# Turning a batch's masks and weights with one transpose, and counting ranks by a scan on VectorE

## The chip, the cores and the metric

The kernel runs on one core of one Trainium2 chip. The metric is the device time of one execution in microseconds (us); the figure that counts is the median of three runs. Five engines work side by side: TensorE (PE; its weight loads are listed as PEld), VectorE (DVE), ScalarE (ACT), GpSimd (POOL) and SyncE (SP). ACT, SP and POOL also issue DMA transfers, each from its own queue.

## The reference

Two layers work on 32 batches of 128 tokens with 1024 features. In the first, each batch is multiplied by a 128x128 matrix that it picks, and the result goes through a mixture of 64 experts, of which each token takes eight. Every expert has room for 256 entries, filled in the order of the tokens:

```python
logits = x @ gate_w.T
w, sel = jax.lax.top_k(probs, K)              # K = 8 of E = 64
w = w / jnp.sum(w, axis=-1, keepdims=True)
oh = jax.nn.one_hot(eid, E, dtype=jnp.int32)
pos = jnp.sum(jnp.cumsum(oh, axis=0) * oh, axis=-1) - 1
valid = pos < CAP                             # CAP = 256
h = silu(inp @ wg) * (inp @ wu); out = h @ wd
```

The second layer is a linear map with adapters per batch and a mixture of eight small experts. The change doesn't touch it.

What matters here is `cumsum`: for each expert, the kernel has to know how many of the tokens up to a given one have chosen it. Together with the weight, that number is what finds the tokens of an expert later.

## The kernel before

The work runs in three stages. **Stage A** (to about 194 us) goes through the 32 batches. For batch `b`, `mixed(b)` multiplies it by its matrix on PE into two `ph` banks, which ACT copies to `hT`; `as_rows(b-1)` turns the batch before it on DVE; `stored(b-1)` writes that to `hbuf` in DRAM from ACT's queue; `logits(b-2)` multiplies `hT` by the gate weights on PE into `plog`; `topped(b-3)` finds the eight largest on DVE. Batches are loaded six ahead by SP (`x`) and POOL (`w`). SP also copies the input to `ybuf`, and in between PE multiplies weights of the second layer (`pcw`, `pcx`, `pcy`, `pcv`). **Stage B** runs the 64 experts: POOL gathers their tokens from `hbuf` (`xin`), PE multiplies, POOL adds the results to `ybuf`. **Stage C** is the second layer.

Every four batches form a group `g` (0 to 7). `powers(g)` and `weights_of(g)` make the weights `wt` from the mask of chosen experts, and `counted(g)`, one iteration later, makes the counts:

- `pcnt`: a matrix of ones times the masks of the four batches gives the number of tokens per expert and batch; DVE adds it up in `upto`.
- for two batches at a time, a bank `prk` of 64 partitions (the experts) holds four blocks of 128 tokens. A product of the mask with `upon`, a fixed matrix of zeros and ones, gives the running count of each expert over the tokens of a batch in their true order; a transpose (a pass with the identity matrix `ident`) gives the weights with experts on partitions.
- ACT copies the bank to `rk_sb` and stores it in `ranks` in DRAM, one row of 2 x 128 numbers per expert and batch: counts first, weights second.

The tokens of a batch lie on the partitions in an order by quarters (token `4i + q` on partition `32q + i`); `upon` takes account of that.

After group 7, `looked_up` finds for each expert slot its batch and the rank sought in it; `fetched` (L307) reads the rows of `ranks` by an indirect DMA into `rkg`; `found` compares, counts and picks the weight; PE's `rows_spread` and DVE's `placed` turn the result into row numbers; and `gathered` (L383) fetches the tokens.

The order on each engine is written out by hand. The wrapper `InOrder` keeps every instruction in the order in which the program text issues it, which is why nearly all rows of the profile carry its line, L219. Each engine works through its own queue in order, and a DMA issue that waits holds up what stands behind it on the same engine. In `counted`, the ACT queue holds copy, store, copy, store; behind it stand the `hT` copies of the next batch. The transfers issued by SP and ACT share eight completion counters in turn.

Of the kernel before, what the change touches and what calls it, by code (L numbers as in the profile page):

```python
# [8 lines left out]
F32 = mybir.dt.float32  # L9
# [3 lines left out]
ALU = mybir.AluOpType  # L13
# [4 lines left out]
P = 128  # L18
# [4 lines left out]
E = 64  # L23
# [9 lines left out]
GB = 4  # L33
# [12 lines left out]
Q = 32  # L46
NQ = P // Q
# [4 lines left out]
def kernel(  # L52
# [22 lines left out]
    nc = tc.nc  # L75

    dram = ctx.enter_context(tc.tile_pool(name="dram", bufs=1, space=DRAM))
    const = ctx.enter_context(tc.tile_pool(name="const", bufs=1))
# [9 lines left out]
    ranks = dram.tile([E, NB + 1, 2, P], F32, name="ranks")  # L88
# [4 lines left out]
    ident = const.tile([P, P], F32, name="ident")  # L93
    make_identity(nc, ident)
    ones = const.tile([P, P], F32, name="ones")
# [5 lines left out]
    iota_t = const.tile([P, P], F32, name="iota_t")  # L101
    nc.gpsimd.iota(
        iota_t, pattern=[[1, P]], base=0, channel_multiplier=0, allow_small_or_imprecise_dtypes=True
# [17 lines left out]
    quad = const.tile([P, 1], F32, name="quad")  # L121
# [4 lines left out]
    inquad = const.tile([P, 1], F32, name="inquad")  # L126
    nc.vector.tensor_scalar(inquad, quad, -float(Q), pcol, ALU.mult, ALU.add)

    mytok = const.tile([P, 1], F32, name="mytok")
    nc.vector.tensor_scalar(mytok, inquad, float(NQ), quad, ALU.mult, ALU.add)  # L130
    upon = const.tile([P, P], F32, name="upon")
    nc.vector.tensor_scalar(upon, iota_t, mytok, None, ALU.is_ge)

    tokrow = const.tile([P, P], F32, name="tokrow")
    nc.gpsimd.iota(
# [64 lines left out]
    def multiplied(n, d, hw, left, pool, tag, pe):  # L200
        w = BLOCKS[n][1] - BLOCKS[n][0]
        pcw = pool.tile([P, 512], F32, name=f"pcw_{n}_{d}", tag=tag)[:, 0:w]
        for j in range(HC):
            if j == HC // 2:
                yield
            pe.matmul(pcw, left[d][:, j, :], hw[:, j, :], start=(j == 0), stop=(j == HC - 1))
        yield pcw
# [5 lines left out]
    class InOrder:  # L213
# [7 lines left out]
    dve, pe, act, pool, sync = (  # L221
        InOrder(e) for e in (nc.vector, nc.tensor, nc.scalar, nc.gpsimd, nc.sync)
    )
# [174 lines left out]
    pa_sm = ppool.enter_context(tc.tile_pool(name="pa_sm", bufs=3, space=PSUM))  # L398
    with (
# [1 line left out]
        tc.tile_pool(name="a6", bufs=6) as a6,  # L401
        tc.tile_pool(name="a2", bufs=2) as a2,
    ):
        xs, ws, hTs, hqs, plogs, tops, lefts_of, exs, masks, wts_of = ({} for _ in range(10))

        def loaded_batch(b):
            ws[b] = a6.tile([P, P], F32, name=f"w_{b}", tag="w_b")
# [53 lines left out]
        def topped(b):  # L461
            g, t = divmod(b, GB)
            if t == 0:
                tops[g] = a2.tile([P, GB, K], F32, name=f"top_{g}", tag="top")
                lefts_of[g] = a2.tile([P, GB, E], F32, name=f"left_{g}", tag="left")
            dve.max(tops[g][:, t, :], plogs[g][:, t, :])
            dve.match_replace(lefts_of[g][:, t, :], tops[g][:, t, :], plogs[g][:, t, :], LOW)
            if t == GB - 1:
                nmax = a2.tile([P, GB], F32, name=f"nmax_{g}", tag="nmax")
                dve.tensor_scalar(nmax, tops[g][:, :, 0], -1.0, None, ALU.mult)  # L470
                masks[g] = a2.tile([P, GB, E], F32, name=f"mask_{g}", tag="mask")
                dve.tensor_scalar(masks[g], lefts_of[g], LOW, None, ALU.is_equal)
                exs[g] = nmax

# [6 lines left out]
                )  # L481

        def weights_of(g):
            wt = a2.tile([P, GB, E], F32, name=f"wt_{g}", tag="wt")
            dve.tensor_tensor(wt, exs[g], masks[g], ALU.mult)
            wsum = a2.tile([P, GB], F32, name=f"wsum_{g}", tag="wsum")
            dve.tensor_reduce(wsum, wt, AX.X, ALU.add)
            rsum = a2.tile([P, GB], F32, name=f"rsum_{g}", tag="rsum")
            dve.reciprocal(rsum, wsum)
            dve.tensor_tensor(wt, wt, rsum.unsqueeze(2).to_broadcast([P, GB, E]), ALU.mult)  # L490
            wts_of[g] = wt

        def counted(g):
            mask, wt = masks[g], wts_of[g]
            pcnt = pf.tile([P, 512], F32, name=f"pcnt_{g}", tag="prow")
            pcnt = pcnt[:, 0 : GB * E].rearrange("p (t e) -> p t e", t=GB)
            pe.matmul(pcnt, ones, mask, start=True, stop=True)
            for t in range(GB):  # L500
                b = g * GB + t
                if b == 0:
                    dve.tensor_copy(upto[:, :, b], pcnt[:, t, :])
                else:
                    dve.tensor_tensor(upto[:, :, b], upto[:, :, b - 1], pcnt[:, t, :], ALU.add)
            for i in range(2):
                rk_sb = a2.tile([E, 2, 2, P], F32, name=f"rk_{g}_{i}", tag="rk")
                prk = pa_sm.tile([E, 2, 2, P], F32, name=f"prk_{g}_{i}", tag="sm")
                for t in range(2):
                    pe.matmul(prk[:, t, 0, :], mask[:, 2 * i + t, :], upon, start=True, stop=True)  # L510
                    pe.transpose(prk[:, t, 1, :], wt[:, 2 * i + t, :], ident)
                act.copy(rk_sb, prk)
                two = slice(g * GB + 2 * i, g * GB + 2 * i + 2)
                act.dma_start(ranks[:, two, :, :], rk_sb)


        def combined(n, d):
# [63 lines left out]
        for b in range(NB):  # L581
# [6 lines left out]
            if b >= 3:  # L588
                topped(b - 3)
            g, t = divmod(b - 7, GB)  # L590
            if t == 0 and g >= 0:
                powers(g)
                weights_of(g)
            elif t == 1 and g >= 0:
                counted(g)
# [21 lines left out]
            if b == 25:  # L617
# [5 lines left out]
                pool.dma_start(ranks[:, NB, :, :], pad)  # L623
        logits(NB - 2)
        counted(NB // GB - 2)
        as_rows(NB - 1)
        stored(NB - 1)
        topped(NB - 3)
        topped(NB - 2)
        last = pair_of_rows(c, rows, sums)  # L630
        next(last)
        logits(NB - 1)
        topped(NB - 1)
        powers(NB // GB - 1)
        weights_of(NB // GB - 1)
        for _ in last:
            pass
        counted(NB // GB - 1)
    part = {0: looked_up([0, 1, 2, 3])}
    fetched(part[0], 2 * NJ)  # L640
# [554 lines left out]
    sm = wts.tile([P, HC, I], F32, name="sm", tag="wu").rearrange("p j i -> p (j i)")  # L1195
# [49 lines left out]
    _, pcw = multiplied(2, HC, hw, lefts, pc_p, "pp", pe)  # L1245
# [140 lines left out]
```

## Time and profile before

| | |
|---|---|
| runs | 2674.31, 2676.79, 2680.87 us (median 2676.79) |
| profiled execution | 2673.54 us, of which the span is 2671.8 us |
| PE busy | 2647.0 us (99%) |
| DVE, ACT, POOL busy | 1867.4 (70%), 547.7 (20%), 1047.3 us (39%) |
| granted PE clock over the span | 0.997 |
| `prk` with `upon` | 64 passes, 323 ns median each |
| `prk` with `ident` | 32 passes, 300 ns median each |
| `rk` copies | 16, 578 ns median |
| `ranks` stores | 16 of 128 KB, 4.8 us median to landing |

Passes on PE overlap, so their own lengths are longer than the distance from one start to the next. A view named the chain follows the work that ended last back from the end; a wait is shown with what released it. A product in float32 appears as two passes, a transpose as one.

### The profile page before, as it was taken

How to read it: one execution, taken by the hardware profiler on the slowest of the kernel's cores; microseconds unless marked ns; L12 is line 12 of the kernel's file. 1: busy time of each engine (PE TensorE's matmuls, PEld its weight loads, DVE VectorE, ACT ScalarE, POOL GpSimd, SP SyncE). 2: the span in 40 equal slices, each digit the busy share in tenths (PEclk: the TensorE clock that was granted, in tenths of full speed). 3: DMA queues.
4: the chain of work that ended last, by engine and by line, in shares of the span. 5: the costliest groups of instructions: out<-in, count | busy, mean ns of one | idle time of the engine just before them, and what ended most of it. 6: DMA issues, size and time to landing. Idle time of an engine off the chain costs nothing.

```text
span 2671.8 us, 25499 instructions
## 1 busy us (share of the span) xinstructions
PE 2647.0 (99%) x8932; PEld 1509.6 (57%) x8932; DVE 1867.4 (70%) x3050; ACT 547.7 (20%) x1174; POOL 1047.3 (39%) x854
## 2 busy tenths in 40 slices
PE   8999999999999999999999999999999999999999
PEld 8985555555555555555555555555555655554554
DVE  4456888888888888888888888878776644444442
ACT  2331222222222222222222222222222100000000
POOL 3106545546455464555555555554441000000000
PEclk9999999999999999999999999999999999999999
DMA  9869788788787887887888878878877322222110
GB/s 349 322 233 369 223 253 264 235 255 265 233 260 249 247 265 232 265 255 240 262 244 251 254 247 250 254 248 250 252 228 211 78 67 67 67 67 67 57 41 33
DMA packets 126367, 568.43 MB, mean 213 GB/s; under 512 B 22928, under 2 KB 48528, under 8 KB 100384
## 3 DMA queue, kind: packets, MB, share of 16 engines
q1 hardware_dynamic: 65664, 383.16, 41.0%
q0 software_dynamic: 52384, 161.60, 24.1%
q10 hardware_dynamic: 8192, 22.06, 2.1%
q8 instruction: 71, 1.16, 0.2%
q14 instruction: 56, 0.46, 0.1%
HBM read 459.68 MB, written 123.83 MB: 218 GB/s over the span
## 4 chain that ended last, share of the span: by engine, by line
PE 96%; DMA 2%; DVE 1%; POOL 1%; issue 0%; SPq 0%; ACT 0%; DVEq 0%; ACTq 0%
PE px L219 27%; PE pr_c L219 18%; PE pv L219 12%; PE py L219 6%; PE ph L219 2%; PE plog L219 2%; PE pth L219 2%; DMA xin<-hbuf,slot_row 1%; PE pcw L219 1%; PE pcx L219 1%; PE prk L219 1%; DMA WB_b<-in_WB 1%; PE pmx L219 1%; PE pcv L219 0%; POOL xin L383 0%
## 5 line engine op out<-in xcount | busy, mean ns | idle before, releaser
L383 POOL DMA_INDIRECT xin<-hbuf,slot_row x512 | 611.5, 1194 | 172.8 <-issue 148.1
L959 POOL DMA_INDIRECT ybuf<-o,slot_tok x128 | 208.0, 1625 | 680.8 <-DVE o L219 229.3
L219 PE MATMUL pr_c<-BM,X 128*128 128x512 f32 x480 | 216.0, 598 | 0.0
L219 POOL DMA_INDIRECT ab<-in_AT,adapter_rows x32 | 36.1, 1128 | 430.7 <-ACT pxw L219 425.2
L307 POOL DMA_INDIRECT rkg<-ranks,row x128 | 153.2, 1197 | 87.6 <-DVE past L219 48.8
L219 PE MATMUL px<-wg,xT 128*128 128x384 f32 x512 | 186.2, 487 | 0.6 <-ACT G_sb L219 0.6
L219 PE MATMUL pv<-t,s 128*128 128x384 f32 x512 | 175.7, 487 | 0.0
L219 PE MATMUL px<-t,s 128*128 128x384 f32 x512 | 175.6, 487 | 0.0
L219 PE MATMUL px<-wu,xT 128*128 128x384 f32 x512 | 175.6, 486 | 0.0
L219 PE MATMUL pv<-wu,s 128*128 128x384 f32 x512 | 175.6, 486 | 0.0
L219 PE MATMUL py<-wg,xT 128*128 128x384 f32 x512 | 175.6, 487 | 0.0
L219 PE MATMUL px<-t,xT 128*128 128x384 f32 x512 | 175.6, 486 | 0.0
L219 DVE TENSOR_TENSOR t<-wu,wg 128x1536 f32<-128x1536 f32 x64 | 113.3, 1770 | 74.2 <-PE pv L219 74.2
L219 DVE STREAM_TRANSPOSE xT<-xin 128x1024 f32<-128x1024 f32 x128 | 151.6, 1220 | 12.9 <-DMA xin<-hbuf,slot_row 10.2
L219 ACT COPY u<-px 128x384 f32<-128x384 f32 x128 | 61.2, 478 | 434.1 <-PE px L219 434.1
L219 PEld LDWEIGHTS pr_c<-BM,X 128*128 128x128 f32 x480 | 89.9, 192 | 101.2 <-issue 101.2
L219 PEld LDWEIGHTS pv<-t,s 128*128 128x128 f32 x512 | 97.4, 190 | 80.8 <-issue 26.0
L219 PE MATMUL pr_c<-ts,ss 128*128 128x512 f32 x320 | 142.4, 593 | 0.0
L219 PEld LDWEIGHTS px<-t,s 128*128 128x128 f32 x512 | 97.5, 190 | 67.6
L219 PEld LDWEIGHTS px<-t,xT 128*128 128x128 f32 x512 | 97.5, 190 | 67.7
L219 PEld LDWEIGHTS py<-wg,xT 128*128 128x128 f32 x512 | 97.5, 190 | 67.7
L219 PEld LDWEIGHTS pv<-wu,s 128*128 128x128 f32 x512 | 97.4, 190 | 67.7
(1570 smaller groups left out, 4553.7 us busy)
## 6 DMA issues: line engine op xcount, KB each, us to landing
wd<-in_wd SPq DMA_DIRECT2D x64, 1536.0 KB, 8.2
wg<-in_wg SPq DMA_DIRECT2D x63, 1536.0 KB, 8.1
wu<-in_wu SPq DMA_DIRECT2D x63, 1536.0 KB, 10.3
hbuf<-hq ACTq DMA_DIRECT2D x32, 512.0 KB, 7.9
ybuf<-in_x SPq DMA_DIRECT2D x32, 512.0 KB, 8.7
xq<-ybuf SPq DMA_DIRECT2D x64, 256.0 KB, 5.1
out_y<-out_c SPq DMA_DIRECT2D x32, 512.0 KB, 2.6
x<-in_x_q SPq DMA_DIRECT2D x28, 512.0 KB, 7.9
```

What stands on the lines that cost most here:

```text
L219: return lambda *args, **kw: kept(op(*args, **kw))
L307: nc.gpsimd.indirect_dma_start(out=some["rk"][:, s, :, :].rearrange("p i t -> p (i t)"), out_offset=None, in_=ranks.rearrange("e b i t -> ...
L383: nc.gpsimd.indirect_dma_start(out=xin[:, q, :], out_offset=None, in_=quarters, in_offset=bass.IndirectOffsetOnAxis(ap=slot_row[:, s : s + ...
L959: nc.gpsimd.indirect_dma_start(out=ybuf, out_offset=bass.IndirectOffsetOnAxis(ap=slot_tok[:, s : s + 1], axis=0), in_=o[j], in_offset=None ...
```

## The change

The masks and the weights of a group are kept in one tile `chosen`, with a batch's mask (64 numbers per token) next to its weights (64 numbers). One transpose of 128 columns per batch then puts the mask on partitions 0 to 63 and the weights on 64 to 127 of `prk`. ACT copies the turned masks to `hits`, bringing the tokens into their true order on the way, and the turned weights to the upper half of `rk_sb`. DVE makes the running counts from `hits` with a scan per batch (each element is the one before it times one plus the mask) into the lower half of `rk_sb`. The two halves go to `ranks` in two stores. `upon` and `mytok` are gone. The contents of `ranks` stay as they were.

Per group, PE has four transposes instead of four products and four transposes; ACT four copies instead of two and four stores instead of two; DVE four scans more.

```diff
-    mytok = const.tile([P, 1], F32, name="mytok")
-    nc.vector.tensor_scalar(mytok, inquad, float(NQ), quad, ALU.mult, ALU.add)
-    upon = const.tile([P, P], F32, name="upon")
-    nc.vector.tensor_scalar(upon, iota_t, mytok, None, ALU.is_ge)
...
-                masks[g] = a2.tile([P, GB, E], F32, name=f"mask_{g}", tag="mask")
+                chosen[g] = a2.tile([P, GB, 2, E], F32, name=f"mask_{g}", tag="mask")
+                masks[g] = chosen[g][:, :, 0, :]
...
-            wt = a2.tile([P, GB, E], F32, name=f"wt_{g}", tag="wt")
+            wt = chosen[g][:, :, 1, :]
...
             for i in range(2):
-                rk_sb = a2.tile([E, 2, 2, P], F32, name=f"rk_{g}_{i}", tag="rk")
-                prk = pa_sm.tile([E, 2, 2, P], F32, name=f"prk_{g}_{i}", tag="sm")
+                rk_sb = a2.tile([P, 2, P], F32, name=f"rk_{g}_{i}", tag="rk")
+                prk = pa_sm.tile([P, 2, P], F32, name=f"prk_{g}_{i}", tag="sm")
                 for t in range(2):
-                    pe.matmul(prk[:, t, 0, :], mask[:, 2 * i + t, :], upon, start=True, stop=True)
-                    pe.transpose(prk[:, t, 1, :], wt[:, 2 * i + t, :], ident)
-                act.copy(rk_sb, prk)
+                    pe.transpose(
+                        prk[:, t, :], chosen[g][:, 2 * i + t].rearrange("p k e -> p (k e)"), ident
+                    )
+                hits = a2.tile([E, 2, P], F32, name=f"hits_{g}_{i}", tag="hits")
+                act.copy(
+                    hits.rearrange("p t (i b) -> p t b i", b=NQ),
+                    prk[0:E].rearrange("p t (b i) -> p t b i", i=Q),
+                )
+                act.copy(rk_sb[E:P], prk[E:P])
+                for t in range(2):
+                    dve.tensor_tensor_scan(
+                        rk_sb[0:E, t, :], ones[0:E, :], hits[:, t, :], 0.0, ALU.mult, ALU.add
+                    )
                 two = slice(g * GB + 2 * i, g * GB + 2 * i + 2)
-                act.dma_start(ranks[:, two, :, :], rk_sb)
+                act.dma_start(ranks[:, two, 1, :], rk_sb[E:P])
+                act.dma_start(ranks[:, two, 0, :], rk_sb[0:E])
```

More of the change, by code (lines that the diff above doesn't have):

```diff
@@ L403 @@
     ):
-        xs, ws, hTs, hqs, plogs, tops, lefts_of, exs, masks, wts_of = ({} for _ in range(10))
+        xs, ws, hTs, hqs, plogs, tops, lefts_of, exs, masks, chosen = ({} for _ in range(10))
         def loaded_batch(b):
@@ L490, in weights_of @@
             dve.tensor_tensor(wt, wt, rsum.unsqueeze(2).to_broadcast([P, GB, E]), ALU.mult)
-            wts_of[g] = wt
         def counted(g):
-            mask, wt = masks[g], wts_of[g]
+            mask = masks[g]
             pcnt = pf.tile([P, 512], F32, name=f"pcnt_{g}", tag="prow")
```

## The prediction

> **What bounds the kernel now.** I read the totals first, then the windows of the first 210 us (all that the diff touches), then the chain in order of time, then the timelines of the engines around it.
>
> ```profile
> PE 2647.0 (99%) x8932; PEld 1509.6 (57%) x8932; DVE 1867.4 (70%) x3050; ACT 547.7 (20%) x1174; POOL 1047.3 (39%) x854
> ```
>
> TensorE is busy 99% of the span; the question is whether that also holds where the change works. The windows (columns: time, then busy us of PE, weight loads, DVE, ACT, POOL, granted clock, DMA share, GB/s) say yes:
>
> ```profile
> 50.00:100.00 50.00, 50.00 (x388) 47.24 (x388) 25.61 (x67) 15.93 (x37) 8.95 (x9) 1.00 0.97 371
> 100.00:150.00 50.00, 50.00 (x388) 47.24 (x387) 24.30 (x64) 16.35 (x38) 9.80 (x11) 1.00 0.87 305
> 150.00:200.00 50.00, 49.26 (x323) 41.45 (x323) 28.71 (x94) 13.96 (x35) 1.15 (x2) 0.93 0.53 206
> ```
>
> DVE and ACT are half busy or less. DMA is at 0.97 early, so it is the next limit. The chain shows one `counted` group (group 1 of 0 to 7; the first column is the start, the second the length):
>
> ```profile
> 70.25 1.73 PE plog L219 x16
> 71.98 0.49 PE pcnt L219 x2
> 72.47 2.37 PE prk L219 x12
> 74.84 1.79 PE ph L219 x16
> ```
>
> No wait stands between these pieces: PE time taken out here is taken from the end, if nothing else then arrives late. The 12 passes of `prk` take 2.37 us in seven groups and 3.89 us in group 6, where the granted clock is 0.50 (174.5 to 181.4 us).
>
> **Part 1, PE.** A group now runs four mask products of two passes and four transposes of one. The timeline has it as a 0.59 us pattern, four times:
>
> ```profile
> 72.99 0.43 PE L219 MATMUL prk<-upon,mask 128*64 128x128 f32 x2
> 73.36 0.30 PE L219 MATMUL prk<-ident,wt 128*64 128x128 f32 x1
> 73.58 0.43 PE L219 MATMUL prk<-upon,mask 128*64 128x128 f32 x2
> ```
>
> Start to start: 0.37 us for a product, 0.22 for a transpose behind one. The change keeps four transposes, now of 128 columns, back to back. Nearest row: the `pth` transposes of the expert stage, also 128x128:
>
> ```profile
> 291.07 0.49 PE L219 MATMUL pth<-ident,h 128*128 128x128 f32 x3
> 291.39 1.46 PE L219 MATMUL px<-wg,xT 128*128 128x384 f32 x4
> ```
>
> Three take 0.32 us from start to start, so four take 0.43; with a little for the change of kind, 0.47. Ends: 0.43 and 4 x 0.23 = 0.92. Saved per group: 2.37 - 0.47 = 1.9 us (1.45 to 1.94).
>
> [...] The trace has one half-clock stretch in the stage, after a gap at 172.3 to 173.0 us, and it cost about 3.1 us (plog 2.28 for 1.73, pcnt 0.96 for 0.49, prk 3.89 for 2.37, pcx 1.97 for 1.37). The other seven groups, a third of whose passes are transposes, ran at 1.00. [...]
>
> **Part 2, ACT, DVE and the new wait.** ACT copied a 64x512 bank in 578 ns. By the `cw` copies (194 elements in 0.32 us, 388 in 0.48) a copy costs 0.16 us + 0.83 ns per element, so each of the two new 256-element copies costs 0.37; the one writing with a stride of four elements is unseen: 0.37 to 0.74, I take 0.37. The scan is unseen too. Rows for its size: 128x128 `past` TENSOR_TENSOR 0.29 us; 256 elements take 0.42 and 512 take 0.69, so 0.16 fixed + 1.04 ns per element. [...] By the row alone 0.29. [...]
>
> The ACT queue now holds two stores per half instead of one, and the second waits for two scans that stand on DVE behind `topped` and four `upto` adds. From T, the end of `pcnt` on PE (72.47 in group 1): DVE's adds end at T+1.2; the first bank's second transpose starts at T+0.12 and lasts 0.30, copies to T+1.23; scans to T+2.05; second store issued to T+2.55 (0.45 each, row `ranks<-rk`); then copies to T+3.4, scans to T+3.9, last store to T+4.45. ACT used to be free at T+3.85 (second `ranks` store 75.49 to 76.32). Queued behind it on ACT: the two `hT` copies of the next batch, its `hbuf` store, and behind these `logits` and the `ph` banks. PE needs the first of those banks when it starts the third batch from there: T + 0.47 + 2 x (1.84 + 1.73) = T+7.6; ACT delivers it at about T+5.2. Cover 2.4 us: cost nothing in groups 0 to 4, though in group 2, where `pair_of_rows` follows one batch later and wants an ACT copy by T+6.7, it comes at T+6.5. Without cover each us is 8 us in all.
>
> The 16 added stores also take turns with SP's in the eight completion counters of the program, where a store waits for the one eight places earlier. In the trace such a wait costs ACT 3 us once, in group 5, amid seven `ybuf` copies:
>
> ```profile
> 162.23 0.58 ACT L219 COPY rk<-prk 64x512 f32<-64x512 f32 x1 [0.59 <-DMA ybuf<-in_x]
> 165.32 0.45 ACTq L219 DMA_DIRECT2D ranks<-rk  x1
> 165.81 1.07 ACT L219 COPY hT<-ph 128x512 f32<-128x512 f32 x2 [3.01 <-DMA hbuf<-hq]
> ```
>
> PE would come there 1.9 us sooner while the DMA does not. The `hT` copies end at 166.9 and PE next needs a bank at 168.7 - 1.9 = 166.8; with one more store in front, about 0.5 us is lost (0 to 2). Doubling the stores doubles packets (512 bytes instead of 1 KB) of only 2 MB: nothing.
>
> **Part 3, the end of the stage.** Group 6 is followed directly by `as_rows(31)`, its store and the last `pair_of_rows`, whose third product must wait for an ACT copy of the first. With ACT's end at T+4.45, the DVE transpose (1.24) and the store, that copy ends near T+5.9; T is 176.3, so the product starts at 182.3 instead of 183.45. Gain 1.1, I take 1.0 (without the half clock in both, a loss of 1: -1 to 2).
>
> Group 7 feeds `looked_up`, the `ranks` fetch, `found`, and PE's `rows_spread`.
>
> ```profile
> 198.55 1.03 POOL L307 DMA_INDIRECT rkg<-ranks,row  x1 [48.85 <-DVE past L219]
> 203.88 0.42 DVE L219 TENSOR_TENSOR hit<-rkg,rank 128x256 f32<-128x256 f32 x1
> 206.75 0.17 DVE L219 TENSOR_TENSOR byq<-quarter,qmask 128x8 f32<-128x8 f32 x1
> 210.10 0.28 PE L219 MATMUL prow<-byq,spread 128*128 128x8 f32 x2
> ```
>
> Now T is 192.25, `byq` is ready at T+14.7 and PE comes at T+18.0 (2.37 + 15.64): 3.3 us of cover. After: PE comes at 0.47 + 15.64 = T+16.1, while DVE starts its look-ups at T+3.9 instead of T+1.24, so `byq` is ready at T+17.4. PE stalls 1.3 us and the gain there is 0.5, not 1.9 (-1 to 1). The gathers behind it keep their distance to PE; the DMA share is 0.99 from 210 to 267 us, so I add nothing and keep 1 us either way.
>
> Costed at nothing: mask tile in pairs (0.29 us may become 0.42, eight times; DVE waits 42.7 us in this stage for `plog`, so it has the room); `mytok` and `upon` dropped at 6 us (PE starts at 8.99, on a weight gather).
>
> **Sum.** Groups 0 to 4: 5 x 1.9 = 9.5; group 5: 1.4; group 6: 1.0; group 7: 0.5; together 12.4 us. The profiled execution took 2673.54 us (span 2671.8 and 1.74 around it), which gives 2661.1. The median of the runs is 3.25 above that execution; the same subtraction gives 2664.4. A measurement can tell about 0.3%, 8 us, from no change.
>
> **Rivals.**
> *Most of it is given back* (2672). DMA at 0.97 to 1.04 between 20 and 70 us and again from 146 to 169 sets the pace, or the stalls of groups 5 to 7 take their upper ends (2 + 3 + 2). For it: DVE waits 10.8 us in all for `hbuf` stores in this stage. Against it: PE itself waits for no DMA between 9 and 172 us, and the batches are loaded six ahead. At 0.9 us kept per group for five groups, 4.5 us.
> *Slower* (2690). ACT's hold passes the 2.4 us cover in every group. Place: `hT` behind the `ranks` store. Point of decision: ACT free at T+8.8 (4.45 + 2.4 of cover + 1.9 saved), which takes scans of 1.5 us, or counter waits of 4.3 us in all groups. At scans of 1.9 us, 8 x 1.6 = 13 us slower. Against it: every row near the scan's size is under 0.5 us, and counter waits of 3 us occur once.
> *More than summed* (2659). Half-clock stretch and the stall at 265 us go: 3 + 2 more. For it: both follow short gaps that depend on when things meet.
> *The change doesn't do it*: the program after has 4 transposes a group for 12 passes, so this is out.
>
> **How the numbers follow.** Sum as forecast (2660 to 2668.5): 0.60. Given back, within 8 us: 0.21. Slower: 0.12. More than summed: 0.07. Faster 0.67, same 0.21, slower 0.12. The range reaches from the last case's 2659 to no change, 2677, leaving out the slower case and a little of the last; the likeliest alone is 2660 to 2668.5.
>
> **What would show it.** In the changed profile: `prk` in the chain at 0.45 to 0.5 us per group; PE still 50.00 of 50 from 50 to 150; the scan at 0.3 to 0.45 us; `prow` first at about 198 us instead of 210.1 with PE idle just before it; in group 6 a PE gap before the second `pcx` piece. Wrong would be: PE gaps before `ph` or `plog` released by ACT in groups 0 to 4, scans over 1 us, or more half-clock stretches than one.

## The result: slower, where a gain was forecast

The changed kernel takes 2685.01 us (median of 8 runs, 2679.34 to 2690.09); the kernel before, run beside it, 2674.9. The ratio is 1.0037, with an interval of 1.0026 to 1.0047: about 10 us slower. The forecast was 2664.4, so it is 20.6 us off and the time lies outside its range.

The profiled execution took 2679.34 us, span 2677.6 (before 2671.8: 5.8 us more). Its totals:

```profile
PE 2633.9 (98%) x8868; PEld 1503.6 (56%) x8868; DVE 1876.8 (70%) x3080; ACT 553.7 (21%) x1190; POOL 1047.2 (39%) x854
```

PE is busy 13.1 us less than before, so the work was saved; it is idle 18.9 us more. The windows say where:

```profile
50.00:100.00 50.00, 45.65 (x357) 44.96 (x357) 29.43 (x77) 16.41 (x39) 8.75 (x9) 0.98 0.97 369
100.00:150.00 50.00, 49.63 (x393) 49.13 (x393) 26.48 (x70) 17.50 (x41) 9.96 (x11) 0.99 0.84 307
150.00:200.00 50.00, 42.77 (x287) 39.00 (x287) 29.52 (x93) 16.89 (x42) 0.00 (x0) 0.93 0.53 199
200.00:250.00 50.00, 43.86 (x136) 24.98 (x134) 28.78 (x71) 4.34 (x9) 28.66 (x27) 1.00 0.90 347
```

From 50 to 100 us PE was busy for 50.00 before and is now for 45.65; from 150 to 200, 42.77 instead of 49.26; from 200 to 250, 43.86 instead of 49.43. The waits of PE in the changed kernel (who waited for whom: us in total, times, longest):

```profile
PE pcx L215 <- ACT cw L215: 6.6, 3, 3.4
...
PE prow L215 <- DVE byq L215: 4.6, 1, 4.6
PE prk L215 <- DVE mask L215: 3.6, 1, 3.6
...
PE plog L215 <- DVE left L215: 1.7, 2, 1.0
```

The waits of `pcx`, `prow` and `prk` did not exist before. With `prow` on `slot_tok` (1.7) and `ph` on a batch (1.0), less 0.7 of `plog` that was there before, and 0.4 more at the first batch, they are 18.9 us. Behind the longest three PE runs at a granted clock of 0.50 to 0.60 for a while (`pcx` takes 2.74 us to the next start instead of 1.42, `prk` 1.11 for 0.44 and `ph` 3.41 for 1.84, the `pv` behind the second `prow` 4.52 for 2.83: about 5.2 us together, where the kernel before lost 3.1). Passes saved: 8 x 1.9 = 15.2. So 18.9 us of waits, 2.1 more of slow clock and 15.2 saved make 5.8 us, the difference of the spans.

**How the gain is lost in group 2.** The chain in group 1 looks as forecast, `prk` at 0.44 us with no gap:

```profile
70.99 0.49 PE pcnt L215 x2
71.48 0.44 PE prk L215 x4
71.92 1.79 PE ph L215 x16
```

One group later ACT's timeline in the kernel before and in the changed one differ (start, length, operation; in brackets the idle time ahead of it and what ended it):

```profile
91.70 0.58 ACT L219 COPY rk<-prk 64x512 f32<-64x512 f32 x1 [3.73 <-DVE left L219]
92.31 0.45 ACTq L219 DMA_DIRECT2D ranks<-rk  x1
92.81 0.58 ACT L219 COPY rk<-prk 64x512 f32<-64x512 f32 x1 [0.53 <-ACT rk L219]
93.42 0.92 ACTq L219 DMA_DIRECT2D ranks<-rk  x1
94.37 0.58 ACT L219 COPY hT<-ph 128x512 f32<-128x512 f32 x1 [0.99 <-PE ph L219]
...
96.87 0.32 ACT L219 COPY cw<-pcx 128x194 f32<-128x194 f32 x1 [1.42 <-PE pcx L219]
```

```profile
89.75 0.62 ACT L215 COPY hits<-prk 64x256 f32<-64x256 f32 x1 [4.71 <-DVE top L215]
90.39 0.37 ACT L215 COPY rk<-prk 64x256 f32<-64x256 f32 x1
90.79 2.62 ACTq L215 DMA_DIRECT2D ranks<-rk  x2
93.45 0.61 ACT L215 COPY hits<-prk 64x256 f32<-64x256 f32 x1 [2.69 <-PE pcx L215]
94.09 0.37 ACT L215 COPY rk<-prk 64x256 f32<-64x256 f32 x1
94.48 2.02 ACTq L215 DMA_DIRECT2D ranks<-rk  x2
96.54 0.59 ACT L215 COPY hT<-ph 128x512 f32<-128x512 f32 x1 [2.09 <-DVE left L215]
...
97.50 0.34 ACT L215 COPY cw<-pcx 128x194 f32<-128x194 f32 x1
```

The first fence is the kernel before. The group's block on ACT, from its first copy to the next `hT`, is 2.67 us long before and 6.79 after. The line to read is the last of the first fence: ACT reached the `cw` copy 1.42 us ahead of PE. The `pcx` that follows on PE needs this copy; its line in the kernel before, then in the changed one:

```profile
97.98 1.48 PE L219 MATMUL pcx<-tc,sc 128*128 128x194 f32 x8
```

```profile
97.90 2.96 PE L215 MATMUL pcx<-tc,sc 128*128 128x194 f32 x8 [3.36 <-ACT cw L215]
```

Before, the copy was done at 97.19, so there was some 0.7 us more of slack on PE's side: 2.1 in all. Without waits PE would now reach this `pcx` 4.9 us sooner (3.0 at `prk` and 1.9 saved in the group), but ACT's block begins only 1.95 sooner, so PE gains 3.0 us on ACT. The block is 4.12 us longer, what follows it 0.1 shorter. 2.1 - 3.0 - 4.1 + 0.1 = -4.9 us. Measured from start to start, PE loses those 4.9 us between `prk` and `pcx`, of which 4.34 show as idle time (0.98 at `plog`, 3.36 at `pcx`).

What fills the longer block is not issue and copies alone. The chain of this stretch shows that the second store of the first half waited for an `hbuf` store issued 10 us earlier, whose data it doesn't touch, on one of the shared counters:

```profile
82.78 9.97 DMA hbuf<-hq
...
92.83 0.58 ACTq L215
```

The scans that this store needed had ended at 91.52, so 1.3 us of the block is this wait:

```profile
90.80 0.72 DVE L215 TENSOR_TENSOR_SCAN rk<-ones,hits 64x128 f32<-64x128 f32 x2
```

The start of `prk` in each group shows the account as it runs (us from the span's start, from PE's timelines; the last kernel is an experiment told of below):

| group | 1 | 2 | 3 | 4 | 5 | 6 | 7 |
|---|---|---|---|---|---|---|---|
| before | 72.4 | 89.5 | 115.8 | 142.1 | 159.2 | 176.2 | 192.2 |
| changed | 71.3 | 86.5 | 117.3 | 142.3 | 161.3 | 177.8 | 192.8 |
| changed, all ranks stores on POOL | 70.6 | 85.7 | 110.3 | 134.7 | 149.8 | 165.8 | 179.5 |

Up to group 2 the changed kernel is 3 us ahead. It loses this and 1.5 us more by group 3, 3.6 us in group 5, and stands at group 7 where the kernel before stood.

### The profile page after: what moved, and what is told of

Its sections match the earlier page's. It is cut to its first block, busy times and chain, and to the rows that moved or that the text cites. A ratio compares the mean times of both kernels' runs of the same rounds, so it can differ in the third digit from the quotient of the medians.

```text
span 2677.6 us, 25451 instructions
## 1 busy us (share of the span) xinstructions
PE 2633.9 (98%) x8868; PEld 1503.6 (56%) x8868; DVE 1876.8 (70%) x3080; ACT 553.7 (21%) x1190; POOL 1047.2 (39%) x854
## 4 chain that ended last, share of the span: by engine, by line
PE 93%; DMA 3%; DVE 2%; issue 1%; ACT 0%; POOL 0%; ACTq 0%; DVEq 0%
PE px L215 27%; PE pr_c L215 18%; PE pv L215 12%; PE py L215 6%; PE pth L215 2%; PE plog L215 1%; PE ph L215 1%; DMA xin<-hbuf,slot_row 1%; PE pcx L215 1%; PE pmx L215 1%; DMA rkg<-ranks,row 1%; DMA ranks<-rk 0%; DMA x<-in_x_q 0%; PE pcv L215 0%; PE pcw L215 0%
## 5 line engine op out<-in xcount | busy, mean ns | idle before, releaser
L215 PEld LDWEIGHTS pr_c<-BM,X 128*128 128x128 f32 x480 | 89.5, 192 | 100.8 <-issue 100.8
## 6 DMA issues: line engine op xcount, KB each, us to landing
wu<-in_wu SPq DMA_DIRECT2D x63, 1536.0 KB, 10.1
x<-in_x_q SPq DMA_DIRECT2D x28, 512.0 KB, 10.1
```

The costliest lines, as they stand in the source:

```text
L215: return lambda *args, **kw: kept(op(*args, **kw))
```

## The experiments

Two theories at first. *Counters*: ACT and SP share eight completion counters in turn (in the changed kernel's trace the `ranks` store issued at 92.83 us has the counter of the `hbuf` store issued at 82.78, eight transfers of the two engines before it), and 16 more stores make each engine wait more often for an older transfer. *Hold*: the store of the counts waits for two scans on DVE while ACT's next copies stand behind it. A third, *end*, says that the look-ups after group 7 come late. Each kernel was timed beside the kernel before on the same chip; that kernel's median differed from chip to chip (2674 to 2683 us), so ratios are compared, or times of one chip. An interval is given behind each ratio.

**Stores split, no scan** (kernel before):

```diff
-                act.dma_start(ranks[:, two, :, :], rk_sb)
+                act.dma_start(ranks[:, two, 1, :], rk_sb[:, :, 1, :])
+                act.dma_start(ranks[:, two, 0, :], rk_sb[:, :, 0, :])
```

> The kernel before, with each ranks store split into two (weights, counts), so 32 stores of the same data instead of 16; products, copies and waits for data are as before. Counter theory (16 more stores make ACT and SP wait longer for the eight shared completion counters, and this alone brings the stalls of groups 2 and 5): slower by 5 to 9 us, with PE gaps between 80 and 170 us. Hold theory (ACT is held because a store waits for scans on DVE between two copies): within 2 us of before, no PE gap before 172 us. End theory (the late look-ups after group 7 cost most): no change, since the look-ups are not moved.

Measured 2681.92, ratio 1.0007 (0.9992 to 1.0021). The profile has a group-5 stall like the changed kernel's (`prk` on DVE's `wt`, 4.5 us), but no measurable loss in the median (the interval reaches from 2 us faster to 6 slower): in the kernel before, twice the stores cost little.

**One store per half, still behind the scan**:

```diff
-                act.copy(rk_sb[E:P], prk[E:P])
+                act.copy(rk_sb[:, :, 1, :], prk[E:P])
...
-                act.dma_start(ranks[:, two, 1, :], rk_sb[E:P])
-                act.dma_start(ranks[:, two, 0, :], rk_sb[0:E])
+                act.dma_start(ranks[:, two, :, :], rk_sb)
```

> The changed kernel, but ACT copies the turned weights to the lower partitions beside the counts, and each half goes out in one store of 1 KB rows, so 16 stores as in the kernel before; the store still waits for the scans. Counter theory: the stalls of groups 2 and 5 (about 5 and 5 us with the slower clock behind them) go, some 8 to 10 us faster than the changed kernel. Hold theory: the store still stands between the copies and waits for DVE; at most 2 or 3 us faster (one issue less per half), the stall of the pair behind group 6 stays near 2 to 3 us. End theory: group 7's store goes out about 0.6 us sooner; 1 us faster.

Measured 2676.62, ratio 0.9985 (0.9975 to 0.9995). The hold is still there and half of the stores are gone; the loss is gone too, and a small gain is left. ACT's block in group 2 is 4.64 us (88.49 to 93.13), PE's wait there 1.21.

**Stores put off** until the next batch's `hT` copies and `hbuf` store are issued, so that none stands waiting for a scan ahead of them:

```diff
-                act.dma_start(ranks[:, two, 1, :], rk_sb[E:P])
-                act.dma_start(ranks[:, two, 0, :], rk_sb[0:E])
+                due.append((two, rk_sb))
...
                 stored(b - 1)
+            ranks_stored()
```

> The changed kernel with its four stores per group put off on ACT's queue behind the hT copies and the hbuf store of the next batch (group 6 behind the last pair of rows, group 7 after its second half), so that ACT makes its four copies in a row and never waits for a scan in front of an hT copy. 32 stores stay. Hold theory: the PE stalls behind groups 2 and 6 go, 6 to 8 us faster than the changed kernel, and group 5's too if it came from the hold, then 10 to 13. Counter theory: the stores only change places; group 5's stall stays, at most 4 us faster. End theory: the end is nearly the same (scans a little sooner), so 3 to 6 us of loss stay behind group 7.

Measured 2695.79, ratio 1.0056 (1.004 to 1.0073): slower still. ACT's timeline of this kernel in group 2:

```profile
97.04 3.50 ACTq L215 DMA_DIRECT2D ranks<-rk  x4
100.58 0.32 ACT L215 COPY cw<-pcx 128x194 f32<-128x194 f32 x1 [4.41 <-DMA ranks<-rk]
```

The four stores now stand right ahead of the `cw` copy and take 3.50 us in a row, although the last scan ended at 95.4. So the hold behind a scan is not needed for the loss.

**Group 7 the old way** (12 passes, no scan, in that group alone):

```diff
+            if g >= NB // GB - 1:
+                for i in range(2):
...
+                        pe.matmul(pro[:, t, 0, :], pair[:, 0, :], upon, start=True, stop=True)
+                        pe.transpose(pro[:, t, 1, :], pair[:, 1, :], ident)
+                    act.copy(ro_sb, pro)
...
+                    act.dma_start(ranks[:, two, :, :], ro_sb)
+                return
```

> The changed kernel, with group 7 alone done the old way (four products and four transposes, one copy and one store per half, no scan). End theory: the look-ups start 3.5 us sooner after the counts, the PE waits for the spread rows (1.7 and 4.6 us) and the slow clock behind the second go, at the price of 1.9 us of PE: 5 to 7 us faster than the changed kernel. Hold and counter theories: the stalls of groups 2, 5 and 6 stay as they are; if they were all of the loss, 0 to 2 us slower than the changed kernel.

Measured 2685.91, ratio 1.0014 (1.0002 to 1.0027); the changed kernel had 1.0037 and 1.0024 on other chips. So the end is worth some 3 to 6 us by the ratios and nothing by the times (2685.0 and 2685.5 there); the two were not measured side by side. No `prow` wait is left in the profile, but PE loses 5.2 us in it in the first expert, waiting for an ACT copy (the last point of this document), which may hide a part of the gain.

**The changed kernel again, and its stores moved to POOL's queue**, on one chip:

```diff
-                act.dma_start(ranks[:, two, 1, :], rk_sb[E:P])
-                act.dma_start(ranks[:, two, 0, :], rk_sb[0:E])
+                pool.dma_start(ranks[:, two, 1, :], rk_sb[E:P])
+                pool.dma_start(ranks[:, two, 0, :], rk_sb[0:E])
```

> The changed kernel once more, so that it stands on the same chip as the three below. All theories: 2682 to 2690 us, ratio 1.002 to 1.005 to the kernel before. The PE waits seen in its first profile come again in groups 2 and 5 (pcx on the ACT copy of cw, 3 us or more; prk on the DVE mask, 3 us or more) and before the second prow piece (about 4 us). If the waits are in other groups, the stalls depend on which eighth-last transfer an engine meets and not on the group.

> The changed kernel with all 32 ranks stores issued from the queue of POOL instead of ACT's; the stores, the copies and the scans are the same. Theory of the counters (the added stores make transfers of ACT and SP wait for one another on eight shared completion counters): the ranks stores leave those counters, the waits of PE for mask (group 5) and for the copy of cw (group 2) go, and the time falls to 2666 to 2672 us, ratio 0.996 to 0.998. Theory of the hold (the second store of a half waits for two scans while ACT's next copies stand behind it): goes with it, as ACT has no stores of ranks; the same time. Theory of the late look-ups (the end): only the two prow waits are left, 6 us in sum, so 2672 to 2676. If the time stays at 2682 or more, neither the counters nor the hold is the cause.

The changed kernel: 2685.54, ratio 1.0024 (1.0009 to 1.004), with `pcx` waits of 8.8 us and `prk` of 4.6. With the stores on POOL: 2668.85, ratio 0.9953 (0.9934 to 0.9972). Moving the 32 stores is worth 16.7 us. The first two windows are full again:

```profile
50.00:100.00 50.00, 50.00 (x391) 49.65 (x391) 30.36 (x82) 17.90 (x42) 12.76 (x16) 1.00 0.94 370
100.00:150.00 50.00, 50.00 (x418) 49.70 (x418) 30.68 (x81) 20.70 (x47) 15.04 (x19) 1.00 0.98 368
```

**One store per half, from POOL** (the two edits above together):

> The changed kernel with the weights copied to the lower 64 partitions, so that a half is one store of 1 KB rows (16 in all, as before the change), issued from POOL. Theory of the counters: no better than the 32 stores from POOL, within 2 us, since neither touches the shared counters (2666 to 2672). If the number of stores matters in another way (POOL's own issue time, about 1 us each, or small packets), 3 us or more better than the 32 stores from POOL.

Measured 2668.42, ratio 0.9952 (0.9935 to 0.997): 16 stores on POOL came out 0.4 us from the 32 (2668.85), the same within the intervals.

**One store per half on ACT, put off** (again both edits):

> The changed kernel with 16 stores of 1 KB rows on ACT (as in the one-store run), each held back until the next batch's hT copies and hbuf store are issued, so that ACT never stands waiting for a scan. Theory of the hold: 4 to 6 us faster than the one-store run's 2676.6 (2671 to 2673). Theory of the counters: within 3 us of it (2674 to 2680), as the same number of stores takes part in the counters.

Measured 2682.22, ratio 1.0005 (0.9988 to 1.0022): 5.6 us slower than with the hold, on another chip and with intervals that overlap, where the hold theory wanted 4 to 6 faster and the counter theory 3 at most either way. It answers neither; like the other deferred run it puts the stores ahead of later ACT copies.

**The kernel before with its stores on POOL**, beside the changed one with its stores there:

```diff
-                act.dma_start(ranks[:, two, :, :], rk_sb)
+                pool.dma_start(ranks[:, two, :, :], rk_sb)
```

> The kernel before with its 16 ranks stores issued from POOL instead of ACT; the 12 passes of prk stay. It tells what of the gain of 32 stores from POOL (ratio 0.9953 for the changed kernel) is the new way of counting and what is the move of the stores. If the move alone brings it: ratio 0.995 to 0.997. If the PE time saved brings it, once nothing stands in its way, as the forecast's sum of 12.4 us has it: ratio 0.999 to 1.001 here, and the changed kernel with the stores on POOL 9 to 13 us faster than this one.

> The changed kernel with 32 stores from POOL again, on the same chip as the kernel before with its stores on POOL: ratio 0.994 to 0.997 to the kernel before.

Measured 2680.26, ratio 0.9985 (0.9972 to 0.9999), and 2668.71, ratio 0.9956 (0.9942 to 0.9971). The move alone brings 1 us in the medians, 0.15% in the ratio. The new way of counting, with the stores off ACT in both, brings 11.5 us: the forecast's sum was 12.4.

**The counters freed in another way**: the stores stay on ACT, the 32 `ybuf` copies leave SP for POOL.

```diff
-            sync.dma_start(ybuf[b * P : (b + 1) * P, :], x[b])
+            pool.dma_start(ybuf[b * P : (b + 1) * P, :], x[b])
```

> The changed kernel with its 32 ranks stores left on ACT behind the scans, and the 32 ybuf copies of 512 KB issued from POOL instead of SP, so that they leave the shared counters. Theory of the counters: what ACT's stores wait for is mostly gone, the waits of PE for cw (group 2) and mask (group 5) shrink from 10 us to under 4 in sum, ratio 0.996 to 1.000. Theory of the hold (the store that waits for the scans holds ACT, whatever the counters do): the waits stay at 8 us or more, ratio 1.002 to 1.005.

Measured 2701.1, ratio 1.007 (1.0056 to 1.0084). The waits for `cw` and `mask` fell to 5.4 us (13.4 in the changed kernel's second profile), but a `prow` wait of 10.9 us appeared and those of `plog` grew to 5.3. The copies now stand on POOL's queue among its gathers; that this is the reason was not tested. A miss for both theories as put.

**Group 7 the old way, stores on POOL**:

> The changed kernel with 32 stores from POOL, and group 7 counted the old way (12 passes, no scan, two stores, from POOL too). Theory of the end: byq comes earlier by the scans and the second copies (about 2 us) while PE reaches it 1.9 us later, so the prow wait of 4.0 us falls to 1 or none and the kernel is 0 to 2 us faster than the same with group 7 the new way. If the prow wait stays at 3 us or more, the fetch of ranks or POOL sets it and not the scans.

Measured 2670.78, ratio 0.995 (0.9936 to 0.9964), beside 2668.71 for the new way in group 7. The `prow` waits are gone and nothing is won. In this profile, the slowest of the five runs, PE waits 4.2 us for another thing in the first expert, so it stays open whether the `prow` waits cost nothing or were traded for this one.

By now it was shown that the stores on ACT take the gain, not by what. Four kernels side by side on one chip. **32 stores of ready zeros added on ACT**, two after each half, to the kernel with its own stores on POOL; **copies in their place**; and **half of the stores on POOL**:

```diff
+                for k in range(2):
+                    at = 2 * (g * GB + 2 * i) + 2 * k
+                    act.dma_start(
+                        spare[:, at : at + 2, :], zeros[0:E, :].rearrange("p (t c) -> p t c", t=2)
+                    )
```

> The changed kernel with its ranks stores on POOL (2669 us, ratio 0.995), plus 32 stores on ACT of a tile of zeros that is ready from the start, two after each half, of the same shape as the ranks stores, into a tensor that nobody reads. They wait for no scan, only for their turn at the shared counters. Theory of the counters: the loss comes back: PE waits for cw and mask of 8 us or more in sum, 2678 to 2686 us, ratio 0.999 to 1.003. Theory of the hold: it stays at 2668 to 2672, ratio 0.994 to 0.997.

```diff
+                for k in range(4):
+                    act.copy(idle, zeros)
```

> The control of the run before: the same, with four ACT copies of 256 elements (about 0.37 us each) after each half in place of the two added stores (0.6 us of ACT's time each). Theory of the counters and theory of the hold: 2668 to 2673, ratio 0.994 to 0.998. If ACT's own time is what was missing: as slow as the run with the stores, ratio 0.999 or more.

> The changed kernel with the 16 stores of counts (those that wait for the scans) on POOL and the 16 stores of weights left on ACT: 16 in the shared counters, none of which waits for a scan. Theory of the counters: as the run with one store per half, 2673 to 2679, ratio 0.997 to 1.000. Theory of the hold: nearly all is back, 2668 to 2671, ratio 0.994 to 0.996.

> The other half: the 16 stores of weights on POOL, the 16 of counts on ACT, where each waits for two scans. Theory of the counters: the same as with the counts on POOL within 2 us, 2673 to 2679. Theory of the hold: as slow as the changed kernel or nearly, 2681 to 2687, ratio 1.000 to 1.003.

Measured: with the ready stores 2677.63, ratio 1.002 (1.0009 to 1.0032); with the copies 2677.36, ratio 1.0003 (0.9992 to 1.0014); counts on POOL 2670.61, ratio 0.9983 (0.9974 to 0.9993); weights on POOL 2671.95, ratio 0.9992 (0.9983 to 1.0). Stores that wait for no scan bring the loss back, which speaks against the hold as the cause; with or without it, 16 stores on ACT come out nearly the same (by its time, 2670.61 us, the run with the counts on POOL lies where the hold theory wanted it, by its ratio where the counter theory did). ACT's timeline with the ready stores, in group 2, shows an `hbuf` store whose counter they wait for; of the 3.45 us, 0.9 is issue:

```profile
89.10 3.45 ACTq L216 DMA_DIRECT2D spare<-zeros  x2
92.65 0.60 ACT L216 COPY hits<-prk 64x256 f32<-64x256 f32 x1 [3.54 <-DMA hbuf<-hq]
```

But copies, which use no counter, bring most of the loss back as well. That was the control, and it went against the theory of the counters.

The control and its base, side by side on one chip:

> The changed kernel with its 32 ranks stores on POOL, beside the next run on one chip. 2664 to 2670 us, ratio 0.995 to 0.998.

> The same with four ACT copies of 0.37 us added after each half (24 us of ACT's time in all, no transfer, no wait). If ACT's own time in these groups is what the changed kernel lacks: 8 to 13 us slower than the run beside it. Theory of the counters, and theory of the hold: within 3 us of the run beside it.

Measured 2670.7, ratio 0.9948 (0.9933 to 0.9964), and 2679.79, ratio 0.9993 (0.9978 to 1.0008). The copies alone cost 9.1 us. ACT's timelines of the two in group 2, without and with them:

```profile
88.02 0.62 ACT L215 COPY hits<-prk 64x256 f32<-64x256 f32 x1 [3.73 <-DVE left L215]
88.66 0.37 ACT L215 COPY rk<-prk 64x256 f32<-64x256 f32 x1
89.06 0.62 ACT L215 COPY hits<-prk 64x256 f32<-64x256 f32 x1
89.70 0.37 ACT L215 COPY rk<-prk 64x256 f32<-64x256 f32 x1
90.09 1.07 ACT L215 COPY hT<-ph 128x512 f32<-128x512 f32 x2
```

```profile
87.93 0.62 ACT L215 COPY hits<-prk 64x256 f32<-64x256 f32 x1 [3.88 <-PE ph L215]
88.58 0.37 ACT L215 COPY rk<-prk 64x256 f32<-64x256 f32 x1
88.97 1.72 ACT L215 COPY idle<-zeros 128x256 f32<-128x256 f32 x4
...
93.47 1.07 ACT L215 COPY hT<-ph 128x512 f32<-128x512 f32 x2
94.44 0.34 ACT L215 COPY cw<-pcx 128x194 f32<-128x194 f32 x1
```

The block is 2.07 us without and 5.54 with the copies, and PE waits 2.12 us for that `cw`.

**What the runs say together.** Ratios of the new way of counting by what stands on ACT: no `ranks` store 0.9948 to 0.9956; 16 stores, with the hold or with none, 0.9983 to 0.9992 (1.0005 put off); 30 or 32 stores 1.0014 to 1.0037 (1.0056 put off, 1.007 with the `ybuf` copies moved); no store but 27.5 us of copies (16 x 1.72) 0.9993 and 1.0003. The loss goes with ACT's time in the group, whatever fills it. The group-2 blocks show it too:

| on ACT | block, us | ratio |
|---|---|---|
| no `ranks` store | 2.07 | 0.9948 |
| 16 stores of weights | 3.34 | 0.9983 |
| 16 stores of counts | 4.52 | 0.9992 |
| one store per half | 4.64 | 0.9985 |
| copies | 5.54 | 0.9993 |
| 32 ready stores | 5.89 | 1.002 |
| 32 stores, the changed kernel | 6.79 | 1.0037 |
| the same again | 8.12 | 1.0024 |

The order is the same but for two pairs of neighbours whose intervals overlap. (In the runs with stores put off, these stand behind the block.) I take ACT's time as the cause.

Two things limit this. First, the ratios rest on the kernel before's own time, which was 2674.0 us beside the four kernels and 2674.9 in the result, but 2680 to 2683 in the other experiments; the changed kernel took 2685.0 and 2685.5 beside 2674.9 and 2681.8. By times alone, the kernel with the counts on POOL (2670.61) equals those with all stores on POOL (2668.4 to 2670.7), so it is not settled what 16 stores cost. What was measured side by side: 16.7 us for the 32 stores, 9.1 for the copies, and 5.4 to 7.0 between the kernels with half of the stores moved and those with ready stores or copies. Second, ACT's time is made of copies, issue and waits. Waits for a shared counter show in the group-2 blocks of the changed kernel (1.3 us) and of the one with ready stores (about 2.5), and those 32 stores, with 0.48 us of issue each in the median, cost no less than 27.5 us of copies; the intervals of those two runs overlap, so how much of the loss is waiting for counters stays open.

The fastest kernels are the changed one with its stores on POOL, 32 or 16 of them: ratios 0.9948 to 0.9956 in four runs, 12.6 to 13.3 us below the kernel before beside them.

## Why the prediction was wrong

*Part 1, PE: right.* 0.47 us for four transposes, measured 0.44 (0.64 in group 0). In group 1 the clock did not drop at the transposes: it was granted at 1.00 from 71.5 to 74.0 us, and the `ph` behind them keeps its 1.79 us. In the table, with the stores on POOL, PE stands at group 7 12.7 us ahead of the kernel before (10.7 to 12.7 in four such profiles); the forecast for groups 0 to 6 was 9.5 + 1.4 + 1.0 = 11.9.

*Part 2, the prices: mostly right.* Contiguous copy 0.368 us (0.37 forecast); scan, in the changed kernel:

```profile
L215 DVE TENSOR_TENSOR_SCAN rk<-ones,hits 64x128 f32<-64x128 f32 x32 | 11.6, 401 | 14.3 <-ACT hits L215 14.3
...
L215 ACT COPY hits<-prk 64x256 f32<-64x256 f32 x16 | 9.8, 615 | 34.0 <-DVE top L215 10.0 <-PE prk L215 9.9 <-PE ph L215 5.0
```

0.40 us in the mean. The forecast's times have 0.41 for each scan (T+1.23 to T+2.05 for two), a length that no run before shows; the row of that size (0.29) was too low. A pair in a row took 0.72 us (90.80 to 91.52). The strided copy takes 0.615, inside the bounds of 0.37 and 0.74, but I had taken the low end. The issue of a store with rows of 512 bytes takes 0.60, where I used the row of the old store with 1 KB, 0.45. In group 1 ACT is free at T+5.9 instead of T+4.45, and PE still doesn't wait, as the cover of 2.4 us there said.

*Part 2, the cover: wrong, and this is the step that failed.* "Cost nothing in groups 0 to 4, though in group 2, where `pair_of_rows` follows one batch later and wants an ACT copy by T+6.7, it comes at T+6.5." I had the copy that decides and a margin of 0.2 us, and costed it at nothing. Measured, that copy ends at T+11.4 (T = 86.48, end at 97.84), 4.9 us after the forecast, and PE waits. Two terms were wrong, by nearly the same amount:

- *The start of ACT's block.* The T+6.5 let it begin right after PE, at T+0.4. In group 2 it begins at T+3.3 (89.75), because the `hbuf` store ahead of it waits for DVE's transpose, which stands behind four sums `sc` of the same iteration (85.58 to 88.19). That, too, was in the timeline before: ACT idle for 3.73 us ahead of the first `rk` copy, which starts 2.2 us after T there.
- *The length of the block.* I had 4.0 us (T+0.4 to T+4.45), and it is 6.79. The strided copies and the dearer issues make 1.1 of the 2.8 us. The rest is waiting, of which I had 0.4 us, for scans: 1.3 us for the shared counter, as shown above, which I had at nothing outside group 5, and 0.8 in the second pair of stores, which takes 2.02 us for 1.2 of issue though its scans ended at 94.82; what held it, the trace doesn't tell.

The `hT` and `cw` copies behind the block took 0.7 us less than forecast. The "slower" rival came nearest in time (2690) and had the right place, ACT's hold ahead of the next copies, but it wanted ACT free after T+8.8 in every group; in group 2 ACT was free at T+10.1, in group 1 at T+5.9.

*Group 5: the size was wrong.* Forecast loss 0.5 us (0 to 2), measured 3.62 at `prk` and 2.2 more of slow clock behind it. By the chain, a `ranks` store of the group before landed 12.68 us after its issue, and the `hbuf` store behind it waited for it:

```profile
144.45 12.68 DMA ranks<-rk
157.17 0.04 issue
157.20 0.33 ACTq L215
157.53 0.04 issue
157.57 0.69 ACT hT L215 x2
```

This is the longest wait for a shared counter in the stage. That 64 KB can take so long was in none of my terms: I costed the doubled stores as packets, at nothing.

*Group 6: right.* From T the third product starts 5.93 us later (177.98 to 183.91); the forecast had 6.0. *Group 7: the first part right.* `byq` at T+17.7 (17.4 forecast), PE at T+16.1 as forecast, a wait of 1.71 us (1.3).

```profile
210.76 0.36 PE L215 MATMUL prow<-byq,spread 128*128 128x8 f32 x2 [1.71 <-DVE slot_tok L215]
```

"The gathers behind it keep their distance to PE" was wrong: the second look-up came late by 4.56 us. It is also where a gain is hard to keep. With the stores on POOL that wait was 3.4 to 6.2 us though everything came earlier, and counting group 7 the old way there, without the wait, brought nothing in the time.

## What to carry to other kernels

Read the slack of an in-order engine at the copy that its consumer waits for (the idle time in front of that copy, and the time from its end to the consumer's start), in the busiest iteration and not in a plain one; ACT was a third busy here, and the slack where it counted was 2.1 us. A saving on the bounding engine spends that slack as surely as added work does: both stand in the same subtraction. Where a change saves passes on PE and pays in copies and stores, send the stores through a queue whose engine has room at that moment (POOL's here, worth 16.7 us), and test that edit with the change before the change is given up.

## What was not expected of the hardware

- A store of 64 partitions with 512-byte rows held ACT's queue for 0.60 us, one with 1 KB rows for 0.45. On POOL the small ones took 0.60 to 0.63.
- The ACT copy with a destination stride of four elements took 0.615 us for 256 elements, the contiguous one 0.368.
- PE gaps of 3.4, 3.6 and 4.6 us were followed by half-clock stretches; gaps of 2.1 and 2.9 us ahead of `pcx` were not. The length alone did not decide: with ready stores PE was idle for 3.1 us between 50 and 150 us, ahead of `pcx`, and the granted clock was 0.95 from 50 to 100 and 0.98 from 100 to 150; with one store per half, put off, the longest gap there was 2.7 us and the clock 0.97 and 0.96; behind gaps of 3.22 (stores put off) and 3.25 us (copies) `pcx` took 1.32 and 1.42 us to the next start, no longer than behind the gap of 2.9 (1.42).
- In five of the twenty profiles ACT was held ahead of a copy in the first expert, the one before its table load, by something that the trace doesn't name, and PE with it in most. It doesn't need the change, since the kernel before with its stores on POOL shows it too:

```profile
264.11 0.48 ACT L219 COPY u<-px 128x384 f32<-128x384 f32 x1 [10.88 <-remote]
264.61 1.28 ACT L219 ACT_TABLE_LOAD   x1
```

In the kernel before's own profile that copy came on time (idle 4.68 us, waiting for PE). PE lost 5.9 us by it here. Whether it is what spreads the runs of one kernel over some 10 us was not tested.
